# Every second x load spread unevenly over the DMA engines of a store-bound kernel

## Chip, cores, metric

One core of one Trainium2 chip. The metric is device time in microseconds, the median of several executions. Ratios are the mean time of one kernel's fast runs over the mean of the other's fast runs of the same rounds, so they are not quite the ratio of the medians quoted beside them.

## The reference

For each of 4096 samples with 32 fields of 64 numbers, and for each of the 496 pairs i < j of fields, field i is multiplied by a 64 x 64 matrix of that pair and the result, element by element, by field j. The output is 520 MB in float32.

```python
idx_i, idx_j = np.triu_indices(32, k=1)
vi = inputs[:, idx_i, :]                      # inputs: 4096 x 32 x 64
vj = inputs[:, idx_j, :]
vidots = jnp.einsum('bpd,pde->bpe', vi, W)    # W: 496 x 64 x 64
return vidots * vj                            # 4096 x 496 x 64
```

## The kernel before

The samples are processed in 16 blocks of 256, two samples a partition. `xs` holds a block of x and is double buffered; the load of the next block is issued by ACT early in the current block, about 80 us ahead of its use. TensorE transposes x and multiplies it; DVE, or ACT with POOL, multiplies by field j and writes the output tile `ot` (three buffers). SP stores each `ot`, 128 partitions of 23 to 27 KB each, 160 times.

```python
def load_x(blk, eng, k0=0, k1=NB):
    src = rows_of(x, blk).rearrange("(p k) f d -> p (k f) d", k=NB)
    eng.dma_start(out=xs[blk][:, 1 + k0 * F : 1 + k1 * F, :], in_=src[:, k0 * F : k1 * F, :])
# ...
for s in range(NBLK * NB * NS):
    # ...
    if st == LATE and kt == 0 and blk and blk + 1 < NBLK:
        new_x(blk + 1)
        load_x(blk + 1, nc.scalar)          # one transfer of 128 rows of 16 KB
    # ... matmuls, multiplications into ot ...
    if pa + m == end:
        nc.sync.dma_start(                  # one output piece of 128 rows
            out=rows_of(out, blk).rearrange("(p k) n d -> p k n d", k=NB)[:, kt, base:end, :],
            in_=ot[:, : end - base, :],
        )
```

## Time and profile before

| | before |
|---|---|
| time, median | 1360.07 us (1359.43 to 1361.06, 3 runs) |
| span of the profiled run | 1357.5 us |
| mean busy share of 16 DMA engines, three queues | 98.0% |
| busiest compute engine | PE, 86% |

The prediction below shows the lines and reads them. One thing goes beyond the page. A trace holds each DMA packet with its start, duration, queue and size, but no engine number. On a busy engine a packet starts 3 or 4 ns before the noted end of the last one (97% of the packets between 60 and 1340 us start so after some other), so the packets can be strung into sixteen chains; the method takes it that each chain runs through the stores in their order. Wherever this document speaks of one engine's rows or gaps, it comes from such chains. The method cannot tell apart engines that are in the same place at the same nanosecond, so the fifteen fast engines swap names at times; the slow one is microseconds behind and keeps its identity. Engines are numbered from 0 in the order in which transfers of few rows fill them; what numbers the hardware gives them no trace shows. The gaps count the packets of the two small instruction queues (8 and 14) as idling, 3.8 us an engine in the mean between 60 and 1340 us. All 170 waits of DVE and POOL for an output buffer (364.8 us) ended only after the sixteenth landing of a store, 0.12 us after it at the median; it came 4.1 us after the fifteenth at the median.

### The profile page before, as it was taken

How to read it: one execution, taken by the hardware profiler on the slowest of the kernel's cores; microseconds unless marked ns; L12 is line 12 of the kernel's file. 1: busy time of each engine (PE TensorE's matmuls, PEld its weight loads, DVE VectorE, ACT ScalarE, POOL GpSimd, SP SyncE). 2: the span in 40 equal slices, each digit the busy share in tenths (PEclk: the TensorE clock that was granted, in tenths of full speed). 3: DMA queues.
4: the chain of work that ended last, by engine and by line, in shares of the span. 5: the costliest groups of instructions: out<-in, count | busy, mean ns of one | idle time of the engine just before them, and what ended most of it. 6: DMA issues, size and time to landing. Idle time of an engine off the chain costs nothing.

```text
span 1357.5 us, 17867 instructions
## 1 busy us (share of the span) xinstructions
PE 1171.5 (86%) x7424; PEld 681.2 (50%) x7424; DVE 951.3 (70%) x1259; ACT 371.1 (27%) x367; POOL 546.2 (40%) x253
## 2 busy tenths in 40 slices
PE   5998988888888888988889888899888889888894
PEld 4554554545455454554545445455454545545552
DVE  5686876767677676766667767677776777767783
ACT  3432322222222222222322222222222322223220
POOL 4544433443333443334434334433344433444441
PEclk9998998989999999998989999999898999999997
DMA  7999999999999999999999999999999999999997
GB/s 291 388 430 431 426 424 431 431 422 426 401 424 413 430 423 412 428 409 431 410 417 425 413 433 407 421 423 410 428 412 424 426 409 424 406 431 428 417 419 335
DMA packets 26128, 562.92 MB, mean 415 GB/s; under 512 B 2896, under 2 KB 2896, under 8 KB 2896
## 3 DMA queue, kind: packets, MB, share of 16 engines
q1 hardware_dynamic: 23744, 529.28, 92.0%
q10 hardware_dynamic: 2304, 32.51, 5.7%
q8 instruction: 58, 0.95, 0.3%
q14 instruction: 22, 0.18, 0.0%
HBM read 41.68 MB, written 520.09 MB: 414 GB/s over the span
## 4 chain that ended last, share of the span: by engine, by line
DMA 50%; PE 23%; DVE 18%; POOL 4%; issue 3%; ACT 0%; DVEq 0%; SPq 0%; POOLq 0%; ACTq 0%
DMA out_dram<-ot 49%; PE ps L192 19%; DVE ot L209 18%; PE ptx L113 4%; POOL ot L207 3%; DMA raw<-in_L_rec_W_dram 1%; POOL rp L94 1%; PE ptw L103 0%; ACT tmp L206 0%; DVE rp L94 0%; DVEq L209 0%; DVE xT L117 0%; ACT wT L106 0%; SPq L211 0%; POOLq L207 0%
## 5 line engine op out<-in xcount | busy, mean ns | idle before, releaser
L209 DVE TENSOR_TENSOR ot<-ps,xs 128x1024 f32<-128x1024 f32 (+15 forms) x1248 | 938.6, 807 | 378.4 <-DMA out_dram<-ot 195.3
L192 PE MATMUL ps<-wT,xT 64*128 64x512 f32 (+14 forms) x6272 | 1025.2, 467 | 118.0 <-DVE ot L209 105.5
L192 PEld LDWEIGHTS ps<-wT,xT 64*128 64x128 f32 x6272 | 554.0, 193 | 554.6 <-DVE ot L209 281.9
L207 POOL TENSOR_TENSOR ot<-tmp,xs 128x1024 f32<-128x1024 f32 x224 | 527.3, 2360 | 623.5 <-ACT tmp L206 397.7
L206 ACT COPY tmp<-ps 128x1024 f32<-128x1024 f32 x224 | 226.7, 1012 | 465.5 <-PE ps L192 460.6
L117 ACT COPY xT<-ptx 128x1024 f32<-128x1024 f32 x127 | 128.5, 1012 | 470.2 <-PE ptx L113 470.2
L113 PE MATMUL ptx<-ident,xs 128*128 128x128 f32 x1024 | 143.8, 285 | 48.9 <-DVE ot L209 34.3
L113 PEld LDWEIGHTS ptx<-ident,xs 128*128 128x128 f32 x1024 | 113.2, 144 | 95.4 <-issue 51.3
L71 POOL MEMSET xs<- 128x64 f32 x16 | 2.4, 151 | 146.7 <-DVE ot L209 146.7
L94 POOL COPY rp<-raw 128x1024 f32<-128x1024 f32 (+1 forms) x7 | 16.1, 2299 | 16.1 <-DMA raw<-in_L_rec_W_dram 11.8
L106 ACT COPY wT<-ptw 128x1024 f32<-128x1024 f32 (+1 forms) x15 | 14.7, 984 | 28.1 <-PE ptw L103 28.1
L103 PE MATMUL ptw<-ident,rp 128*128 128x128 f32 (+1 forms) x128 | 17.0, 280 | 3.2 <-DVE rp L94 2.0
L94 DVE COPY rp<-raw 128x1024 f32<-128x1024 f32 (+1 forms) x9 | 11.0, 1233 | 12.3 <-DMA raw<-in_L_rec_W_dram 11.9
L103 PEld LDWEIGHTS ptw<-ident,rp 128*128 128x128 f32 (+1 forms) x128 | 14.1, 145 | 10.2 <-issue 5.6
L106 ACT ACT_TABLE_LOAD x1 | 1.3, 1283 | 1.2 <-PEq L229 1.2
L117 DVE COPY xT<-ptx 128x1024 f32<-128x1024 f32 x1 | 1.2, 1208 | 0.0
L106 DVE COPY wT<-ptw 128x1024 f32<-128x1024 f32 x1 | 1.2, 1208 | 0.0
masks.py:197 POOL MEMSET ident<- 128x128 f32 x1 | 0.2, 205 | 0.3 <-POOLq L229 0.3
masks.py:199 POOL TENSOR_SCALAR_AFFINE_SELECT ident<-ident 128x128 f32<-128x128 f32 x1 | 0.3, 292 | 0.0
L229 POOL MEMSET const-float32-0.0<- 128x1 f32 x1 | 0.1, 98 | 0.2 <-issue 0.2
L229 POOL MEMSET const-bfloat16-1.0<- 128x1 bf16 x1 | 0.1, 101 | 0.0
L229 POOL MEMSET const-uint8-127<- 128x1 uint8 x1 | 0.1, 101 | 0.0
(1 smaller groups left out, 0.1 us busy)
## 6 DMA issues: line engine op xcount, KB each, us to landing
out_dram<-ot SPq DMA_DIRECT2D x64, 3360.0 KB, 16.2
out_dram<-ot SPq DMA_DIRECT2D x64, 2880.0 KB, 16.7
out_dram<-ot SPq DMA_DIRECT2D x32, 3392.0 KB, 17.2
xs<-in_r_inputs_dram ACTq DMA_DIRECT2D x15, 2048.0 KB, 16.6
raw<-in_L_rec_W_dram SPq DMA_DIRECT2D x3, 2048.0 KB, 15.6
raw<-in_L_rec_W_dram SPq DMA_DIRECT2D x1, 1792.0 KB, 15.7
xs<-in_r_inputs_dram ACTq DMA_DIRECT2D x1, 1024.0 KB, 11.4
xs<-in_r_inputs_dram SPq DMA_DIRECT2D x1, 1024.0 KB, 17.7
```

The costliest lines, as they stand in the source:

```text
L71: nc.gpsimd.memset(xs[blk][:, 0, :], 0.0)
L94: copy(rp[:r], src[:, k * EU : (k + 1) * EU])
L103: nc.tensor.transpose(pt[:, n, :r], rp[:r, n].rearrange("p h d -> p (h d)"), ident[:r, :r])
L106: copy(wT[c][:, :, k * EU : (k + 1) * EU], pt[:, :, :r].rearrange("p e r -> p r e"))
L113: nc.tensor.transpose(pt[:, n, :], xs[blk][:, s : s + 2, :].rearrange("p f d -> p (f d)"), ident)
L117: copy(xT, pt)
L192: nc.tensor.matmul(ps[:, h, lo - pa : hi - pa, :], xT[blk, kt, n // RUN][h * D : (h + 1) * D, n % RUN, :], wT[c][h * D : (h + 1) * D, lo - ...
L206: nc.scalar.copy(tmp, src)
L207: nc.gpsimd.tensor_mul(dst, tmp, xj)
L209: nc.vector.tensor_mul(dst, src, xj)
L229: nc = _bacc.Bacc("TRN2", target_bir_lowering=False, num_devices=1)
```

## The change

Its intent: the output stores keep all DMA engines nearly full (98.0%), so a load that puts more rows on some engines and fewer on others should relieve those that are late. The pieces of 21, 7 and 4 rows are meant to run on seven, seven and four engines; in the prediction k is that number for a transfer. Before the change this was the author's assumption: all transfers of the kernel before, of 128 and 112 rows, have sixteen landings.

```diff
-    def load_x(blk: int, eng, k0: int = 0, k1: int = NB):
+    def load_x(blk: int, eng, k0: int = 0, k1: int = NB, parts=((0, P, 1),)):
         src = rows_of(x, blk).rearrange("(p k) f d -> p (k f) d", k=NB)
-        eng.dma_start(out=xs[blk][:, 1 + k0 * F : 1 + k1 * F, :], in_=src[:, k0 * F : k1 * F, :])
+        for a, b, step in parts:
+            eng.dma_start(
+                out=xs[blk][a:b:step, 1 + k0 * F : 1 + k1 * F, :],
+                in_=src[a:b:step, k0 * F : k1 * F, :],
+            )
+    UNEVEN = ((0, P, 2), (1, P, 4), (3, 84, 4), (87, 112, 4), (115, P, 4))
@@
-            load_x(blk + 1, nc.scalar)
+            load_x(blk + 1, nc.scalar, parts=UNEVEN if blk % 2 else ((0, P, 1),))
```

## The prediction

> **What bounds the kernel now.** I read the busy shares, the slices, the DMA queues, the stretches by window, the waits and the issues, in that order, and then the packet records and landing times that the trace holds beneath them.

> ```profile
> PE 1171.5 (86%) x7424; PEld 681.2 (50%) x7424; DVE 951.3 (70%) x1259; ACT 371.1 (27%) x367; POOL 546.2 (40%) x253
> ...
> DMA  7999999999999999999999999999999999999997
> ...
> q1 hardware_dynamic: 23744, 529.28, 92.0%
> q10 hardware_dynamic: 2304, 32.51, 5.7%
> q8 instruction: 58, 0.95, 0.3%
> ```

> The page: no compute engine is full, and the DMA digit is 9 in all slices but the first and last. Queue 1 (outputs and weights) and queue 10 (x, issued by ACT) fill 97.7% of the time of 16 DMA engines. Output traffic is what the kernel is bound by; a DVE or PE that waits less gains nothing.

> ```profile
> 60.00:300.00 240.00, 213.38 (x1349) 123.67 (x1348) 174.47 (x232) 64.77 (x64) 95.63 (x44) 0.96 1.00 427
> 300.00:600.00 300.00, 261.80 (x1677) 151.16 (x1675) 215.45 (x288) 80.96 (x80) 119.41 (x54) 0.98 0.99 420
> ...
> 1200.00:1340.00 140.00, 124.95 (x800) 73.28 (x800) 103.81 (x139) 37.45 (x37) 58.82 (x25) 0.96 0.98 419
> ```

> The busy time by stretch: stretch and its length, then PE, PEld, DVE, ACT and POOL with instruction counts, then granted clock, DMA share, GB/s. After 300 us the DMA share slips from 1.00 to 0.99 and 0.98, and the rate from 427 to 420 GB/s. The stores still wait:

> ```profile
> DVE ot L209 <- DMA out_dram<-ot: 195.3, 97, 5.2
> POOL ot L207 <- DMA out_dram<-ot: 169.5, 73, 5.6
> ```

> The waits (total us, times, longest): DVE and POOL wait for an output buffer to come free, up to 5 us, while the average DMA engine is idle for 1 to 2%. A buffer is free only when all 16 engines have finished their rows of it, so I looked for one late engine. The landing times of one transfer's 16 parts show it: transfer 168 of 181 lands for 15 engines within 2.2 us and for the last at 6.2 us after the first; transfer 181 within 1.6 us and at 5.1 us. The landing spread averages 4.6 us over all transfers. It is always one.

> The packet records (start, duration, queue, bytes; no engine number) let me follow each engine: on a busy engine the next packet starts 3 or 4 ns before the noted end of the last. Followed through from 60 to 1340 us, one engine has 0.6 us of gaps; the other fifteen have 21 to 23 us each, mean 22.2. The slow one is no more loaded; its output rows take longer: 882.6 against 859.0 ns for 23,040 bytes (496 rows), 1033.4 against 1019.1 ns for 26,880 bytes (497 rows), 1042.6 against 1010.1 ns for 27,136 bytes (248 rows). That is 11.7 + 7.1 + 8.1 = 26.9 us, which agrees with 22.2 us of idling plus about 5 us by which the others end early. Its x rows cost what the others' do: 617 against 618 ns. So **one DMA engine paces the kernel**, and the time moves one for one with its work until another engine is as late.

> [...]

> **The change part by part.** The late x load runs for blocks 1 to 14 and is uneven for odd ones: 7 loads of 14.

> ```profile
> L75 ACTq EVENT_SEMAPHORE  x30: 17/38/1576, 56.2 to 1180.5; - x30
> L75 ACTq DMA_DIRECT2D xs<-in_r_inputs_dram x16: 334/342/408, 0.7 to 1182.1; - x16
> ...
> DMA to landing us min/median/max: 11.4/16.6/18.3
> ```

> *Rows per engine in one load.* Before: 128 rows over 16 engines, 8 each. After: 64 rows on 16 engines, 4 each; 32 on 16, 2 each; 21 on k = 7, 3 each on engines 0 to 6; 7 on k = 7, 1 each on 0 to 6; 4 on k = 4, 1 each on 0 to 3. Engines 0 to 3 have 4+2+3+1+1 = 11 rows, 4 to 6 have 10, 7 to 15 have 6. Check: 44 + 30 + 54 = 128.

> *What it removes.* If the slow engine is one of 7 to 15: 2 rows x 7 loads x 617 ns = 8.6 us, all on the path that sets the end.

> *What it moves.* Engines 4 to 6 gain 2 x 7 x 618 ns = 8.7 us, engines 0 to 3 gain 3 x 7 x 618 ns = 13.0 us. This lies beside the slow engine's work as long as they keep a lead. Their room before is 22.2 us of idling plus some 5 us of lead at the end, about 27 us. Closing in from both sides takes 8.6 + 13.0 = 21.6 us of it: some 5 to 6 us stay, so they don't become the bound on average. Within one load they fall back by 5 rows, 3.1 us, against a lead of 5 to 6 us; the slow engine's disadvantage, 26.9 us over some 15.6 blocks or 1.7 us a block, gives back 3.4 us by the next uneven load. It fits, narrowly.

> *What it adds.* Four issues more on ACT, 4 x 342 ns = 1.4 us a load, 9.6 us in all, on an engine that is 27% busy: off the path. Completion packets: 16 + 16 + 7 + 7 + 4 = 50 instead of 16 a load, of 9 ns each; engines 0 to 3 have 4 more, 0.25 us in the run. The bytes are the same. The data is due a block (some 82 us) later and lands in about 17 us, so a later landing hurts nobody.

> *Sum.* 1360.07 - 8.6 = 1351.5 us; I add half a microsecond[...]: **1352.0 us**, 0.6% less.

> **The rivals.** *The slow engine is one of the first seven.* Then it gains rows: +13.0 us (1373) among 0 to 3, +8.6 us (1369) among 4 to 6. For: the profile names no engine; and among 31 packets that start in the same nanosecond as another of their queue the slow one's is listed first 22 times, which would suit a low number if the list is in engine order, which I can't establish. Against: [...]the intent of a change that deliberately loads the first seven. I give it 0.15.

> *Engines 0 to 3 become the bound.* If their lead is used up in each uneven load, the landing is theirs and part of the gain goes: 1354 to 1358. For: only 5 to 6 us of room. Against: room enough by the sum, and the issue of a piece is some 6 us ahead of the slow engine's need of it (transfer 181 is issued at 1342.1, transfer 180 lands on the slow engine at 1348.5). 0.15.

> *A fixed ceiling shared by the engines.* If all 16 share one limit, evening the load gives nothing: 1360. For: 427 to 431 GB/s looks like a plateau. Against: fifteen engines do idle, and a median 26,880-byte row takes 996 ns, which is also the fastest one seen[...]. 0.05.

> *New waits on ACT.* Five issues in a row hold up ACT's copies of transposed x and its evictions by 1.4 us a load; PE would feel it, the stores have the 6 us above. Under 1 us in all.

> **Range and chances.** Main case, about 0.65: 1350.5 to 1353. Partial gain: 1354 to 1358. Nothing: 1360. Slow engine among the first seven: 1369 to 1373. Run to run the kernel before spans 1359.4 to 1361.1, so the noise is about a microsecond. The range 1349 to 1361 leaves out the wrong-side case only. Two per cent is 27 us, three times all that can be moved: faster by over 2% 0.01, within 2% 0.98, slower 0.01.

> **What would show it right or wrong.** Queue 10 should hold 2304 + 7 x 34 = 2542 packets and the same 32.51 MB; the share of q1 should rise from 92.0% to about 92.6%, as the same packets fit a shorter span; the x issues should show 8 of 2048 KB and 7 each of 1024, 512, 336, 112 and 64 KB. DVE's wait for the outputs (195.3 us) should fall by some 5 to 10 us, and the last landing of a transfer should trail the first group by less than now after an uneven load. Wrong would be: a spread that grows at each uneven load (the slow engine is among the first seven); five to seven engines landing last together (they became the bound); x rows well over 620 ns[...]; or an ACT that waits long before the later four issues.

## The result and the profile after

The changed kernel took 1369.38 us (1368.69 to 1373.69, 4 runs) against 1360.57 us for the kernel before (4 runs): ratio 1.0073, 95% interval 1.0051 to 1.0094. It is 8.8 us slower, where 8.1 us less had been predicted.

The DMA lines of the page after (busy tenths and packets, then by queue: packets, MB, share of 16 engines' span):

```profile
DMA  7999999999999999999999999999999999999997
...
DMA packets 26366, 562.92 MB, mean 412 GB/s; under 512 B 3134, under 2 KB 3134, under 8 KB 3134
...
q1 hardware_dynamic: 23744, 529.28, 91.5%
q10 hardware_dynamic: 2542, 32.51, 5.6%
```

Queue 10 has exactly the 2542 packets foretold for the same 32.51 MB, so the transfers were cut as worked out. But the shares fell where they should have risen: 91.5% of 1367.6 us is as much store time as 92.0% of 1357.5 us (1251 and 1249 us). The same work stands in a longer span, so the mean engine idles more. Busy time by stretch shows little of it (stretch, length, PE, PEld, DVE, ACT, POOL with counts, clock, DMA share, GB/s):

```profile
60.00:300.00 240.00, 210.51 (x1324) 121.75 (x1322) 171.92 (x228) 63.64 (x63) 92.50 (x43) 0.96 1.00 423
300.00:600.00 300.00, 264.85 (x1670) 152.95 (x1666) 213.28 (x285) 81.12 (x81) 122.94 (x55) 0.95 0.98 416
```

Up to 600 us the rate is 4 GB/s lower than before, from 600 to 900 us the same (418), then 4 lower and 3 higher. The chains of packets say whose idling it is. All packets from 30 us on, us:

```
                     store and W rows   x rows          gaps over 0.1 us   ends at
before  slow engine   1287 in 1253.7    120 in  74.0     1.5               1356.0
        others, mean  1287 in 1227.2    120 in  74.4    22.3               1351.3
after   slow engine   1287 in 1253.9    134 in  83.9     0.6               1365.7
        others, mean  1287 in 1230.7    119 in  73.6    28.3               1360.5
```

There is still exactly one engine without gaps; the next one has 23 us of them between 60 and 1350 us. Its stores take what they took. It loads 14 x rows more, and ends 9.7 us later, for 9.9 us more of x rows. Load by load, the sixteen chains of each uneven load hold 11, 11, 11, 11, 10, 10, 10 rows and nine times 6, and the slow one holds 10 in all seven. So it is one of the three engines that load 10 rows, engines 4 to 6 as numbered here: with the transfers of 7 and 21 rows, without those of 4. The change gives work to the engine that it should have relieved.

The slow engine is slow in nearly all its rows, not in a few. In the kernel before, its median store rows of 23,040, 26,880 and 27,136 bytes take 879, 1029 and 1043 ns, those of the others 855, 996 and 1006 ns, about 3% less each time. The means of the 26,880-byte rows lie closer together, as the other engines' first rows of such a transfer are long (1116 ns in the mean, up to 1.6 us).

The waits moved too (waiter, waited for: us in total, times, longest):

```profile
POOL ot L215 <- ACT tmp L214: 458.0, 120, 15.4
...
DVE ot L217 <- PE ps L200: 188.1, 232, 3.1
DVE ot L217 <- DMA out_dram<-ot: 180.1, 96, 5.2
...
POOL ot L215 <- DMA out_dram<-ot: 139.6, 65, 5.6
```

DVE and POOL together wait 45 us less for output buffers than before (319.7 against 364.8 us), in a slower kernel. Before, POOL waited 397.7 us for ACT and DVE 156.9 us for PE; these waits grew. The view of the loading line shows what holds ACT up:

```profile
L76 ACTq DMA_DIRECT2D xs<-in_r_inputs_dram x44: 340/550/2243, 0.7 to 1191.3; - x44
```

Issues (ns: least, median, most) had been 334/342/408. The records in their order have medians of 532 ns for 64 rows, 503 for 32, 1289 for 21, 1817 for 7 and 1440 for 4: 5.6 us a load in which ACT issues nothing else. The even loads still issue in 345 ns. The time went with the place in the series, not with the number of rows: over all runs below but the last, the third to sixth issue of a series take 1.3 to 2.0 us at the median, for 4 to 21 rows, while 14 rows in second place (staircase) take 0.32 us, and 4 or 2 rows in seventh place, after a pause of some 3 us, take 0.58 and 0.64 us. ACT's products come later, and part of the wait for buffers is waited elsewhere: even4 below, cut but with equal rows, shows the same shift (POOL for ACT 439.1 us, DVE for PE 199.8, both for buffers 315.7). The slow engine's 0.6 us of gaps says that this cost nothing here: the stores stayed ahead of it.

The column of time to landing is empty for this kernel, since some of its transfers land in fewer than 16 parts (8, 8 and 5 landings are noted for 21, 7 and 4 rows, one more than the engines counted; what the one more is, no trace shows); landing spreads are not compared.

### The profile page after: what moved, and what is told of

Its sections match the earlier page's. It is cut to its first block, busy times and chain, and to the rows that moved or that the text cites. A ratio compares the mean times of both kernels' runs of the same rounds, so it can differ in the third digit from the quotient of the medians.

```text
span 1367.6 us, 17923 instructions
## 1 busy us (share of the span) xinstructions
PE 1176.6 (86%) x7424; PEld 683.7 (50%) x7424; DVE 953.7 (70%) x1259; ACT 371.3 (27%) x367; POOL 546.2 (40%) x253
## 2 busy tenths in 40 slices
DMA  7999999999999999999999999999999999999997
## 3 DMA queue, kind: packets, MB, share of 16 engines
q1 hardware_dynamic: 23744, 529.28, 91.5%
q10 hardware_dynamic: 2542, 32.51, 5.6%
## 4 chain that ended last, share of the span: by engine, by line
DMA 51%; PE 23%; DVE 18%; POOL 4%; issue 3%; ACT 1%; DVEq 0%; SPq 0%; POOLq 0%; ACTq 0%
DMA out_dram<-ot 50%; DVE ot L217 18%; PE ps L200 18%; PE ptx L121 4%; POOL ot L215 3%; DMA xs<-in_r_inputs_dram 1%; PE ptw L111 1%; POOL rp L102 1%; ACT tmp L214 0%; DVEq L217 0%; DVE rp L102 0%; ACT wT L114 0%; SPq L219 0%; POOLq L215 0%; DVEq L246 0%
## 5 line engine op out<-in xcount | busy, mean ns | idle before, releaser
L102 POOL COPY rp<-raw 128x1024 f32<-128x1024 f32 (+1 forms) x7 | 15.4, 2206 | 16.5 <-DMA raw<-in_L_rec_W_dram 10.6
L111 PE MATMUL ptw<-ident,rp 128*128 128x128 f32 (+1 forms) x128 | 18.1, 294 | 2.5 <-DVE rp L102 1.3
```

The lines of the kernel that those rows point to most:

```text
L102: copy(rp[:r], src[:, k * EU : (k + 1) * EU])
L111: nc.tensor.transpose(pt[:, n, :r], rp[:r, n].rearrange("p h d -> p (h d)"), ident[:r, :r])
```

## The experiments

**Theory A**: one DMA engine among 4 to 6 has longer store rows, paces the kernel, and each x row added to it adds 0.62 us. **Rival B**: the cutting costs (ACT held, rows at partition steps, more packets). **Rival C**: engines 0 to 3, with 11 rows, became the bound. The first three runs shared a chip, the next four another, the last used a third.

The engine counts that the expectations give to the small transfers fit queue 10's packets in every run: 34 more than before for each load of the change's five parts (2780 in every_load), 32 for the staircase's (2752), 48 for the parts of even4 (2640), mark4 (2640) and first4 (2640, 2832 and 2976 for 7, 11 and 14 loads), each transfer adding as many as the engines given for it.

About one run in five or six (12 of 66; of first4_eleven none of five), of the kernel before too (1364.5 to 1364.8 us in three of eleven runs), is some 5 us longer. Where the profile fell on such a run the second slice of the DMA digits has an 8 and everything after it is shifted. In every_load:

```profile
DMA  7899999999999999999999999999999999999997
```

Medians are little touched by it, but the ratios, being of means, are. In both profiled long runs (every_load and mark4) one copy of the weights on DVE, begun at 46 to 47 us, takes 5.0 us, where the same copy takes 1.0 us in the kernel before. Why it does is not known.

### even4: the cutting without the unevenness

```diff
-    UNEVEN = ((0, P, 2), (1, P, 4), (3, 84, 4), (87, 112, 4), (115, P, 4))
+    UNEVEN = ((0, P, 2), (1, P, 4), (3, 64, 4), (67, P, 4))
```

> The odd x loads are cut in four transfers of 64, 32, 16 and 16 rows at the same partition steps, all on 16 engines: 8 rows an engine again. Theory A (one of the engines 4 to 6 is slow and paces the kernel; the row count does it): as before, 1360 us, within 2. Rival B (the cutting itself costs: ACT held by more issues, rows at partition steps, more completion packets): most of the +8.8 us stays, 1365 us or more.

Measured: 1361.23 us (6 runs) against 1359.99 us (11 runs), ratio 1.001, interval 0.9989 to 1.0031. Each chain holds 8 rows; the slow engine has 0.6 us of gaps, the others 18.9. The issues of 16 rows, though on all engines, took 1.85 us at the median, so ACT was held 4.7 us a load. Steps, packets and ACT's hold remain and the loss is gone, to within 1 to 2 us by the medians and 4 us by the interval. Rival B does not explain 8.8 us.

### every_load: twice the dose

```diff
-            load_x(blk + 1, nc.scalar, parts=UNEVEN if blk % 2 else ((0, P, 1),))
+            load_x(blk + 1, nc.scalar, parts=UNEVEN)
```

> The five-part load in all 14 late loads instead of 7. Theory A: the slow engine carries 28 rows more than before, 28 x 0.62 = +17.3 us: 1377.5 us; the slow engine still idles under 2 us, the others about 35 us. Rival C (engines 0 to 3, with 11 rows, became the bound): they gain 42 rows, +26 us, so 1386 us or less, and several engines without idle time. Rival B (cost of cutting): also double, but then the slow engine has idle time of its own.

Measured: 1378.12 us (5 runs) against 1359.99, ratio 1.0132 (1.0111 to 1.0154): +18.1 us for 28 rows, 0.65 us a row, after +8.8 for 14. In the profile, a long run, the engine with the fewest gaps (2.6 us between 60 and 1350 us) loads 10 rows in every uneven load; the others have 12 us or more. Rival C wanted four engines with 11 rows and no gaps. Its time, 1386 us or less, would admit 1378; the chains do not, and it is out for this kernel.

### staircase: which engine

```diff
-    UNEVEN = ((0, P, 2), (1, P, 4), (3, 84, 4), (87, 112, 4), (115, P, 4))
+    UNEVEN = ((0, 96, 1), (96, 110, 1), (110, 115, 1), (115, 121, 1), (121, P, 1))
...
+            load_x(blk + 1, nc.scalar, parts=UNEVEN)
```

> All 14 late loads in parts of 96, 14, 5, 6 and 7 rows: engines 0 to 4 load 10 rows, engine 5 loads 9, engine 6 loads 8, engines 7 to 13 load 7, engines 14 and 15 load 6. Theory A says which engine is the slow one by the time and by the rows that it is seen to load: engine 4: 10 rows, 1360.6 + 28 x 0.62 = 1377.9 us; engine 5: 9 rows, 1369.2 us; engine 6: 8 rows, 1360.6 us. Rival (no single slow engine among these): any other number of rows on the engine that never idles.

Measured: 1396.63 us (4 runs), ratio 1.0265 (1.0237 to 1.0293), outside all three forecasts of time. The row count still answers: the slow engine loads 10 rows each time, 6 of the 96 and one of each smaller transfer, so it is among engines 0 to 4, and with the 10 rows in the change and in every_load (engines 4 to 6) only engine 4 is left. This takes it that transfers of few rows fill the engines in one order in all these kernels; mark4 below needs only its own counts. The excess of 19 us over the 1377.9 us for engine 4 is shown by the queues:

```profile
q1 hardware_dynamic: 23744, 529.28, 90.4%
q10 hardware_dynamic: 2752, 32.51, 6.1%
```

Of a span of 1394.9 us these are 1261 and 85 us an engine, where the kernel before had 1249 and 77 for the same bytes. The x rows of the late loads took 677 ns instead of 617 on the slow engine, and its 26,880-byte rows 1054 instead of 1032. The expectation had kept the row's cost fixed. This kernel had dropped the partition steps: its 96 rows lie in one contiguous group, 6 an engine.

### mark4: engine 4 alone with its row count, at partition steps

```diff
-    UNEVEN = ((0, P, 2), (1, P, 4), (3, 84, 4), (87, 112, 4), (115, P, 4))
+    UNEVEN = ((0, P, 2), (1, P, 4), (3, 64, 4), (67, 84, 4), (87, 104, 4), (107, 120, 4), (123, P, 4))
```

> Odd loads in transfers of 64, 32, 16, 5, 5, 4 and 2 rows at partition steps: engines 0 and 1 load 11 rows, 2 and 3 load 10, engine 4 alone 9, engines 5 to 15 load 7. Theory A4: the engine that never idles is seen to load 9 rows in each of these loads, and the time is 1360.2 + 7 x 0.62 = 1364.5 us. Rival D (engine 5 or 6): it loads 7, 1355.9 us. Rival E (one of 0 to 3): 10 or 11 rows, 1369 us or more.

Measured: 1366.26 us (4 runs) against 1359.79 us (11 runs), ratio 1.0054 (1.0041 to 1.0067). In six of the seven loads the engine without gaps holds 9 rows, a count that only one chain has. In the first load, at 117 us, it was still level with others and its chain holds 11, so its identity isn't certain there. It is the engine reached by transfers of 5 rows and not by those of 4: the fifth. The x rows cut at steps took 615 ns in the mean over all engines, not 679 as in the staircase. The time is 2 us above the expectation.

### first4_odd, first4_eleven, first4_all: relieving engine 4

```diff
-    UNEVEN = ((0, P, 2), (1, P, 4), (3, 84, 4), (87, 112, 4), (115, P, 4))
+    UNEVEN = ((0, P, 2), (1, P, 4), (3, 64, 4), (67, 80, 4), (83, 96, 4), (99, 112, 4), (115, P, 4))
...
     first4_odd:     parts=UNEVEN if blk % 2 else ((0, P, 1),)
     first4_eleven:  parts=UNEVEN if blk % 4 else ((0, P, 1),)
     first4_all:     parts=UNEVEN
```

Four transfers of 4 rows put 4 rows more on engines 0 to 3; the others have 7.

> Odd loads in seven transfers of 64, 32, 16, 4, 4, 4 and 4 rows at partition steps: engines 0 to 3 load 11 rows, engines 4 to 15 load 7. Theory A4 (engine 4 is the slow one): it sheds 7 rows, 7 x 0.62 = 4.3 us: 1355.9 us. Rival D (the slow one is 5 or 6): the same here. Rival E (the slow one is among 0 to 3): 7 x 3 x 0.62 = +13 us, 1373 us. Rival B (ACT's longer hold, about 9 us a load, costs time): above 1360 us.

Measured: 1357.42 us (6 runs) against 1359.79, ratio 0.999 (0.9978 to 1.0002): 2.4 us less by the medians, of 4.3 expected, and by the ratio not clear of zero. In the profile the slow engine holds 7 rows in every uneven load and ends at 1353.1 us, 2.9 us before its end in the kernel before: its x rows take 4.2 us less, its stores 2.1 us more (1255.8 against 1253.7 us). Why the stores took longer is not known; in even4, too, they took about 2 us more.

> The same seven transfers in 11 of 14 late loads. Theory A4: the slow engine sheds 11 rows, -6.8 us: 1353.4 us; engines 0 to 3 take 33 rows, +20.4 us, of about 27 us of room: still not the bound. Rival C (engines 0 to 3 become the bound earlier than the sum says): 1356 us or more.

Measured: 1355.43 us (5 runs), ratio 0.997 (0.9958 to 0.9982), the fastest kernel. Here five chains run almost without gaps (0.0, 0.8, 1.2, 1.8 and 3.7 us; the next 20.9), and the one with fewest has 11 rows in the uneven loads. So engines 0 to 3 have now become as late as engine 4, and a little later. The gaps of 0.0, 1.2, 1.8 and 3.7 us belong to the chains with 11 rows and are packets of the instruction queues; counted as work, they leave these four idle for 0.1 us or less. The four end at 1350.9 to 1351.4 us, where engine 4 alone would have ended at 1356.0 - 6.8 = 1349.2 us (an estimate). That is the 2 us by which the time lies above the 1353.4 expected: rival C, in part.

> The same in all 14 late loads. The slow engine sheds 14 rows, -8.6 us; engines 0 to 3 take 42 rows, +26 us, which is their whole room. If the room of 27 us is right, the two meet: about 1354 to 1360 us, no better than with 11 loads, and five engines idle little. If there is more room than that: 1351.6 us.

Measured: 1363.42 us (6 runs), ratio 1.0029 (1.0017 to 1.0041). Four chains have gaps of 0.3, 1.5, 3.6 and 5.6 us, the next 19.9. The one with fewest holds 11 rows: engines 0 to 3 are the bound, and engine 4 waits for them. Rival C was false for the change and is true here. The time is 3 us above the range expected. ACT now waits for earlier x transfers, which it does not do in the kernel before:

```profile
ACT tmp L214 <- DMA xs<-in_r_inputs_dram: 92.8, 9, 11.8
```

This does not explain the 3 us. With the packets of the instruction queues counted as work, the four chains idle for 0.1 us or less between 60 and 1340 us, so nothing that ACT does held them up; and first4_eleven, the fastest, has 72.0 us of such waits. What the four have more is work: 42 x rows each, and stores of 1229.7 us in the mean, against 1227.2 us for the fast engines before.

### mark4_out48: the engine or the partitions

```diff
-                nc.sync.dma_start(... [:, kt, base:end, :], in_=ot[:, : end - base, :])
+            for r0, r1 in ((0, 48), (48, P)):
+                nc.sync.dma_start(... [r0:r1, kt, base:end, :], in_=ot[r0:r1, : end - base, :])
```

(on top of mark4, the arguments shortened)

> As mark4, and each output piece stored by two transfers, of partitions 0 to 47 (3 rows an engine) and 48 to 127 (5 rows an engine)[...]. Theory F (the engine is slow, whatever it stores): the engine with the slowest rows still loads 9 rows in the odd x loads, its 26,880-byte rows some 1 to 3% above the others' mean. Rival G (the partitions it stored are slow to read): the slow rows are now spread over other engines, and no engine stands out with 9 rows. The time may be longer in both[...]; it decides nothing.

Measured: 2031.69 us, a single run of unknown state, against 1360.24 us.

```profile
DMA  8999999999999999989999899998999989999997
...
DMA packets 29027, 562.95 MB, mean 277 GB/s; under 512 B 5792, under 2 KB 5792, under 8 KB 5792
...
q1 hardware_dynamic: 26304, 529.29, 90.4%
q10 hardware_dynamic: 2640, 32.51, 3.9%
```

The engines are nearly as busy and move a third less: 90.4% of 2029.9 us is 1835 us of store time an engine for the same bytes. A row of 23,040 bytes took 1266 ns in the mean, 853 at best. All store rows suffer so much that no slow engine could be picked out. Each half ran on sixteen engines: queue 1 has 26,304 packets against 23,744, 16 more for each of the 160 pieces. That the division gave engine 4 other partitions was the assumption; no trace shows which partitions an engine reads. The run is inconclusive on its question: whether engine 4 is slow or what it reads is stays open. It does show what this division cost here, half as much again for each store row. Whether the other partitions did it or the doubled number of transfers, it can't say.

## Why the prediction was wrong

- *"One DMA engine paces the kernel"*: right. It holds in the kernel after, in every_load and in mark4: one chain without gaps, and time follows its rows.
- *Rows an engine, 11, 10 and 6*: right, counted in all seven loads.
- *"What it removes. If the slow engine is one of 7 to 15"*: this is the step that failed. I gave it 0.85, on an assumption that no trace of this kernel showed and on the intent of the change. The trace had not placed the engine, and the one hint in it, the order of packets of the same nanosecond (22 of 31 times first), pointed to a low number; I discounted it. If the list is in engine order, which no run shows, engine 4 would be first in 11 of 15 such pairs (22.7 of 31, an estimate by counting), one of 7 to 15 in 8 of 15 at most (16.5). The slow engine is the fifth, engine 4. The sign of the term turns: not -8.6 but +8.6 us.
- *The first rival, "+8.6 us (1369) among 4 to 6"*: that is what happened, 1369.4 us. It was worked out beforehand to within half a microsecond and given 0.15, and the range left it out; the mistake was the 0.15.
- *Cost of a row, 617 ns*: nearly right. The slow engine's x rows took 9.9 us more for 14 rows. 8.6 of this is the count; the rest is x rows that took 626 ns in the mean instead of 617.
- *"4 x 342 ns = 1.4 us a load"*: the added issues were mis-sized. The five took 5.6 us a load against 0.34, as the third to fifth took 1.3 to 1.8 us each. Off the path it was: 0.6 us of gaps on the slow engine, and even4, with 4.7 us of issues a load, cost 1 us or nothing.
- *Room of about 27 us for engines 0 to 3*: right to within 2 us. In first4_eleven 20.4 us added to them and 6.8 taken from engine 4 make 27.2 us, and the four are then some 2 us later than engine 4 would be: the room was about 25. The idling of 22.2 us had counted the packets of the instruction queues.
- *"A fixed ceiling shared by the engines"*: out. The same bytes took 1355.4 to 1378.1 us, following the rows of one engine or of four.
- *"The landing spread averages 4.6 us"*: taken in order of issue, the sixteen landings of the 181 transfers spread over 5.1 us in the mean. Nothing rests on it.
- *DVE's wait for the outputs*: a bad indicator. It fell by 15 us in a slower kernel, and by 30 us in even4 at nearly the same time.

What stays open: why engine 4's store rows are longer while its x rows are not, and why the stores take about 2 us longer in even4 and in first4_odd. Whether engine 4 or what it reads is slow was not shown either.

## What to carry to other kernels

When all engines of a queue look full, look for the one that has no gaps, and before work is shifted away from it, find out which one it is: mark each with a different amount of work in one run and count. A sum of several terms is worth nothing while the sign of its largest one rests on an assumption that the trace doesn't confirm. After relief, stop where the next engines have become as late: here 11 of 14 loads gained 0.3%, all 14 lost 0.3%.
